# A graph-network kernel on one core: degree sums taken from the attention's tiles, twelve adjacency tiles kept, x loaded in pieces, key loads with other strides

## The chip, the cores and the metric

The kernel runs on one core of a Trainium2 chip. The time is the device time of one execution in microseconds, and what counts is the median of several runs.

## The reference, cut to what matters

Four layers work on 3327 nodes with 128 features and one adjacency matrix of zeros and ones. Each layer takes the layer norm of x, clips it at zero and adds its result to x.

- Layer 0: `x1 = swish((adj @ h) @ W + b)`, then the same once more with x1 in place of h. Two products with the whole adjacency.
- Layer 1: attention with 128 heads of 8 features: `softmax(q k^T * scale + adj + adj)`, times v, and an output projection. The adjacency is added twice, so the kernel adds its double.
- Layer 2: `adj @ states`, a message layer and a GRU cell.
- Layer 3: a normalised product with `d = 1 / sqrt(sum(A, axis=-1))`, distances between all nodes, the four nearest, and a second normalised product. Only here are the sums of the adjacency, the degrees, needed.

## The kernel before

Nodes stand in T = 26 slots of P = 128 partitions (`NP` = 3328, one more than N = 3327). The adjacency is read as its transpose `adjT`: tile t holds 128 source nodes (127 in the last tile) and a row of 3327 destination nodes, 1.7 MB in float32. A sum over a node's neighbours is therefore a sum over partitions and tiles.

The front of the program and the attention each stand in a manual schedule: every engine's instructions, and the DMA issues on SP's queue, keep the order in which the program writes them. PE is TensorE, DVE is VectorE, ACT is ScalarE, POOL is GpSimd, and SP issues DMAs.

**Layer 0.** `load_x` (L95) brings x in three DMAs by groups of partitions. Layer norm goes over three pieces of slots (`cuts`, L331) in stages `centre`, `spread`, `scaled`, and splits h into two float16 parts. The first product (L410 to L421) loads the 26 tiles through three buffers (`load_a`), multiplies both parts with the upper 16 bits of the tile (L373), and calls `look_at` (L401): DVE adds the tile to `colsum` (L405), and ACT sums the lower 16 bits of each number (L407). Ten tiles, `KEPT` (6, 8, ... 24), are also cast to bfloat16 by ACT (L419) and stay in SBUF. For half of them DVE collects all bits into `most` (`every_bit`).

The second product (L455 to L484) runs over `order`: the loaded tiles, with a kept tile after every two. Each loaded tile is read by PE, by DVE for its greatest value (`a_max`, L465), and by POOL, which writes its first 476 columns, doubled and in bfloat16, for the attention (`doubled`, L270 to L278). Between these stand seven products of ones with `colsum` (L477), copied by ACT into a row, which goes to DRAM and back as `deg` (one degree per partition and slot). In its midst SP loads x once more, with nodes in another order (`x_r`, L482 to L484). Four kept tiles, `TAIL`, are multiplied last, column chunk by column chunk.

**Projections.** `project_rows` (L616) runs over 26 blocks of rows and stores q, k and v in DRAM. From the fifth block on, a list `early` of steps is worked off beside it: raw loads of the keys of the first two head groups (`load_raw`, L688), one DMA for each head, whose rows are copied four times; queries and values; their parting into a rounded part and a rest (`split_rows`, whose sign and zero pattern comes from bits 8 and 16 of the partition number, L745); and the first tiles' exponentials.

**Attention.** Queries go in seven chunks of 476 columns (`q_chunks`, `QW`), heads in 32 groups of four, and keys in 26 tiles. The loop (L869 to L911) has one step per chunk c, group g and tile t; a tile pair shares one buffer `p8`. For an even tile PE makes four score products in the four `early` banks (L816), and DVE adds the doubled adjacency to them (L819). For an odd tile three products go to `late`, one of which PE also adds the adjacency to (L835), and the fourth to an `early` bank and DVE. ACT takes the exponential of the three (L837); POOL multiplies two of them by the exponential of the adjacency (L839); ACT takes the exponential of the other five (L840). `weigh` multiplies with the values six steps later (L847), and at a group's last tile DVE copies the result to `o4` (one buffer, L856), which four DMAs store. `key_pair` copies two tiles of keys (L603) on DVE at each odd tile but one.

The doubled tiles of chunk c + 1 are made while chunk c runs. At step t = 6 SP loads the next of the 26 tiles (`load_adj`), in at most one group a tile; at step t = 22 POOL doubles it (L908), after that step's scores in the program's order:

```python
if t == max(T - 4, 3) and c + 1 < len(q_chunks):
    for a, i, w in a_in:
        a_next.append(doubled(adj_pools[(c + 1) % 2], a[: rows_of(i), :w], i, w))
        to_store.append((c + 1, i, a_next[-1]))
```

`tail` (L984) holds layers 2 and 3 and the attention's output projection; `deg` is first used at L1030. A second, general path (L1289 on) runs only where the data do not fit the fast one; it does not run here.

## Time and profile before

| | |
|---|---|
| median of 3 runs | 10946.24 us (10944.75 to 10950.41) |
| profiled execution | 10958.07 us |
| its span, first to last instruction | 10956.4 us |
| busy PE / DVE / ACT / POOL | 97% / 95% / 93% / 66% |
| front: layer 0 and projections | 0 to 486 us |
| attention | 486 to about 10200 us |
| output projection, layers 2 and 3 | the rest |
| L819, adds of the adjacency on DVE | 14560 times, 646 ns each |
| L840, exponentials of five tiles on ACT | 2912 times, 2633 ns |
| L837, exponentials of three tiles on ACT | 2912 times, 1801 ns |
| L839, products on POOL | 2912 times, 2173 ns |
| L603, copies of keys on DVE | 2681 times, 552 ns |

A line of a timeline gives the start in us, the duration, the engine, the line of the kernel, the operation, what it writes and reads, and how often it is repeated; in brackets stands how long the engine was idle before it, and who ended that. Durations of instructions that follow each other on one engine overlap, so the distance between their starts is what each one costs. A line of windows gives start and end, the length, the busy time of PE, PE's weight loads, DVE, ACT and POOL with the number of instructions, the granted TensorE clock as a share of the full one, the DMA share and the GB/s.

### The profile page before, as it was taken

What the parts mean: (1) busy time and instruction counts of PE and PEld (TensorE: products, weight loads), DVE (VectorE), ACT (ScalarE), POOL (GpSimd) and SP (SyncE); (2) the same over time, 40 slices, a digit from 0 to 9 for tenths busy, and PEclk for the clock granted to TensorE, in tenths of its full rate; (3) what the DMA queues carried; (4) which work ended last, traced back from release to release, by engine and by line L of the source; (5) the groups of instructions that cost most, each with busy time, mean ns of one, the idle gap of its engine ahead of it and who ended that gap; (6) DMA issues with size and microseconds to landing.
All of it is one profiled execution on the core that took longest, in us unless ns stands there. A gap on an engine that the chain in (4) does not pass through costs nothing.

```text
span 10956.4 us, 201911 instructions
## 1 busy us (share of the span) xinstructions
PE 10591.0 (97%) x76701; PEld 3116.0 (28%) x76740; DVE 10354.7 (95%) x18137; ACT 10140.6 (93%) x6324; POOL 7260.8 (66%) x4298
## 2 busy tenths in 40 slices
PE   6899999999999999999999999999999999999897
PEld 2322222222222222222222222222222222222453
DVE  7699999999999999999999999999999999999665
ACT  4599999999999999999999999999999999999432
POOL 2278887777777777777777777777777766666203
PEclk8999999999999999999999999999999999999998
DMA  7655555433433433433343343343333333333422
GB/s 275 206 123 128 125 120 118 69 63 67 70 63 64 70 65 64 70 65 63 69 68 63 64 70 64 64 71 63 62 68 67 62 61 63 56 62 59 149 99 99
DMA packets 420289, 928.18 MB, mean 85 GB/s; under 512 B 67713, under 2 KB 349201, under 8 KB 385004
## 3 DMA queue, kind: packets, MB, share of 16 engines
q1 hardware_dynamic: 416058, 908.63, 40.7%
q8 instruction: 606, 9.93, 0.4%
q0 software_dynamic: 3248, 6.53, 0.2%
q14 instruction: 377, 3.09, 0.1%
HBM read 775.17 MB, written 139.72 MB: 84 GB/s over the span
## 4 chain that ended last, share of the span: by engine, by line
ACT 74%; issue 9%; PE 9%; DVE 3%; POOL 1%; DMA 1%; SPq 0%; DVEq 0%; ACTq 0%; POOLq 0%
ACT p L837 44%; ACT p L840 28%; PE acc L847 3%; DVE p L819 1%; PE agg_ps L228 1%; PE early L816 1%; ACT e L519 1%; PE late L816 1%; PE late L835 1%; PE yp L1026 0%; POOL rows L1242 0%; DVE idx L1218 0%; DVE top L1217 0%; SPq L593 0%; ACT oT L1023 0%
## 5 line engine op out<-in xcount | busy, mean ns | idle before, releaser
L819 DVE TENSOR_TENSOR p<-early,a 128x476 f32<-128x476 f32 (+1 forms) x14560 | 8414.3, 646 | 115.2 <-PE early L816 83.6
L839 POOL TENSOR_TENSOR p<-p,e 128x952 f32<-128x952 f32 (+2 forms) x2912 | 6326.6, 2173 | 2653.5 <-ACT p L837 2247.5
L840 ACT ACTIVATE p<-p 128x2380 f32<-128x2380 f32 (+1 forms) x2912 | 7667.2, 2633 | 0.0
L847 PE MATMUL acc<-p,v 128*9 128x476 f32 (+1 forms) x46592 | 5739.6, 564 | 22.4 <-DVE o L856 5.5
L837 ACT ACTIVATE p<-late 128x1428 f32<-128x1428 f32 (+1 forms) x2912 | 5243.6, 1801 | 20.7 <-PE late L835 19.0
L816 PE MATMUL early<-q,k 32*128 32x476 f32 (+1 forms) x14560 | 3714.1, 479 | 27.3 <-DVE p L819 8.2
L816 PEld LDWEIGHTS early<-q,k 32*128 32x128 f32 x14560 | 1579.4, 181 | 2752.6 <-DVE p L819 2690.1
L603 DVE CAST k<-k_in 128x256 fp32r<-128x256 f32 x2681 | 1479.3, 552 | 0.0
L816 PE MATMUL late<-q,k 32*128 32x476 f32 (+1 forms) x8736 | 1416.4, 479 | 52.0 <-ACT p L837 51.9
L816 PEld LDWEIGHTS late<-q,k 32*128 32x128 f32 x8736 | 547.5, 181 | 2378.2 <-ACT p L837 2265.5
L835 PE MATMUL late<-a,two_i 128*128 128x476 bf16 (+1 forms) x3072 | 1124.0, 374 | 0.0
L847 PEld LDWEIGHTS acc<-p,v 128*9 128x9 f32 x46592 | 692.6, 88 | 1347.5 <-issue 1257.5
L835 PEld LDWEIGHTS <-two_i 128*128 128x128 bf16 x3072 | 281.0, 96 | 665.1 <-issue 665.1
L228 PE MATMUL agg_ps<-a,part 128*128 128x512 bf16 (+1 forms) x1067 | 242.2, 379 | 49.4 <-issue 43.1
L373 PE MATMUL agg_ps<-a,part 128*128 128x512 bf16 (+2 forms) x714 | 175.6, 402 | 87.0 <-DMA a<-in_adjT_dram 63.0
L187 ACT COPY agg<-agg_ps 128x512 f32<-128x512 f32 x9 | 4.7, 594 | 255.8 <-PE agg_ps L228 255.8
L277 POOL TENSOR_SCALAR a<-a_in 128x476 bf16<-128x476 f32 (+2 forms) x156 | 240.0, 1539 | 0.5
L603 POOL CAST k<-k_in 128x256 fp32r<-128x256 f32 x231 | 203.1, 880 | 0.0
L1211 PE MATMUL sp<-yT,hT 128*128 128x512 f32 (+1 forms) x364 | 170.6, 610 | 12.4 <-ACT agg L1216 6.5
L228 PEld LDWEIGHTS <-part 128*128 128x128 f16 x1092 | 109.5, 101 | 177.1 <-issue 76.0
L1127 POOL TENSOR_TENSOR xs_late<-xs_late,b_s 128x3328 f32<-128x3328 f32 x1 | 7.3, 7252 | 227.4 <-DVE ln_xc L157 227.4
L856 DVE COPY o<-acc 105x476 f32<-105x476 f32 (+1 forms) x224 | 144.7, 646 | 6.6 <-PE acc L847 5.8
(284 smaller groups left out, 2615.8 us busy)
## 6 DMA issues: line engine op xcount, KB each, us to landing
k_in<-kt SPq DMA_DIRECT2D x1776, 207.9 KB
v<-vd SPq DMA_DIRECT2D x896, 117.0 KB
a<-in_adjT_dram SPq DMA_DIRECT2D x40, 1663.5 KB
a<-adj SPq DMA_DIRECT2D x78, 831.8 KB
q<-qt SPq DMA_DIRECT2D x1520, 29.8 KB
a_in<-in_adjT_dram SPq DMA_DIRECT2D x125, 238.0 KB
adj<-a SPq DMA_DIRECT2D x156, 119.0 KB
vd<-v_st SPq DMA_DIRECT2D x25, 576.0 KB
```

The lines of the kernel that those rows point to most:

```text
L228: nc.tensor.matmul(acc[c][:, :w], part[:, t, :], a[:, c0 : c0 + w], start=(t == 0 and i == 0), stop=(t == T - 1 and i == len(parts) - 1),)
L277: nc.gpsimd.tensor_scalar(a2[:kp, :w], a, 2.0, None, op0=ALU.mult)
L373: nc.tensor.matmul(acc[c][:, :w], part[:kp, t, :], a16[:kp, c0 : c0 + w], start=(n == 0 and i == 0), stop=(last and i == len(parts) - 1),)
L603: engine.tensor_copy(k, slots(k_in)[:, t : t + 2, :])
L816: nc.tensor.matmul(sp[:, :we], k[r, t % 2, :], q4[r, :we], start=True, stop=stop)
L819: nc.vector.tensor_tensor(p8[:, PLACES[t % 2][i], :we], sp[:, :we], a2[:, :we], op=ALU.add)
L835: nc.tensor.matmul(late[:, i, :we], two_i, a2[:, :we], start=False, stop=True)
L837: nc.scalar.activation(p8[:, 5:8, :we], late[:, :, :we], AF.Exp)
L839: nc.gpsimd.tensor_tensor(g8, g8, e_a[:, :we].unsqueeze(1).to_broadcast([P, n_g, we]), op=ALU.mult)
L840: nc.scalar.activation(p8[:, :5, :we], p8[:, :5, :we], AF.Exp)
L847: nc.tensor.matmul(acc[32 * i : 32 * i + EA, :w], v4[:kp, i, t, :], p8[:kp, PLACES[t % 2][i], :w], start=(t == 0), stop=(t == T - 1),)
L1211: nc.tensor.matmul(sp[:, c0 : c0 + w], slots(zT)[:, t, :], z2T[:, cols], start=True, stop=False)
```

## The change

- The degrees are no longer summed from the float32 tiles in layer 0. `add_to_sum` adds each doubled tile to `deg_half` [128 x 476]. For chunk 0 POOL does it, during the second product, right after each doubling. For chunks 1 to 6 DVE does it, right after the doubling in the attention's step t = 22 (the first tile of each chunk is copied by POOL instead). `store_sum` multiplies ones with `deg_half`, halves the row and writes it to DRAM: for chunk 0 in the second block of the projections, for chunk c at step t = 5 of its own first group, through an `early` bank and an `o4` buffer. `deg` is read back at the beginning of `tail` in the program; in SP's queue the load stands in the second group of the last chunk.
- `KEPT` has twelve tiles (2, 4, ... 24). `a_max` of the other fourteen and `every_bit` of all twelve are taken by DVE in the first product. In the second product DVE reads no tile. 14 tiles are loaded there instead of 16.
- The first three loads of the second product stand ahead of everything else, the loads of `x_r` follow them at once, and the fourth load comes after these.
- `load_x` goes by pieces of slots (0 to 2, 2 to 8, 8 to 26), which the first layer norm takes too.
- `load_raw` writes a head's eight rows with the four copies of each row next to each other, and a step of the list loads all four heads of a group; the sign pattern takes bits 1 and 2. The list has 16 steps instead of 22.

The general path keeps a sum of its own, which is left out below.

```diff
--- before.py
+++ after.py
@@ -92,10 +92,14 @@
     tiny_c = const.tile([P, 1], F32, name="tiny_c")
     nc.vector.memset(tiny_c, 1e-10)
 
+    X_CUTS = (0, 2, 8, T)
+
     def load_x(dst):
         nc.vector.memset(dst[96:P, T - 1, :], 0.0)
-        for p0, p1, n in ROW_PARTS:
-            nc.sync.dma_start(dst[p0:p1, :n], dram(x_in, p0 * T * D, [[T * D, p1 - p0], [D, n], [1, D]]))
+        for t0, t1 in zip(X_CUTS, X_CUTS[1:]):
+            for p0, p1, n in ROW_PARTS if t1 == T else ((0, P, t1),):
+                n = min(n, t1) - t0
+                nc.sync.dma_start(dst[p0:p1, t0 : t0 + n], dram(x_in, (p0 * T + t0) * D, [[T * D, p1 - p0], [D, n], [1, D]]))
 
     weights = const
 
@@ -277,6 +281,22 @@
         nc.gpsimd.tensor_scalar(a2[:kp, :w], a, 2.0, None, op0=ALU.mult)
         return a2
 
+    degd = dpool.tile([1, NP], F32, name="degd")
+    deg_half = const.tile([P, QW], F32, name="deg_half")
+
+    def add_to_sum(engine, a2, c, first=False):
+        w = q_chunks[c][1]
+        if first:
+            nc.gpsimd.tensor_copy(deg_half[:, :w], a2[:, :w])
+        else:
+            engine.tensor_tensor(deg_half[:, :w], deg_half[:, :w], a2[:, :w], op=ALU.add)
+
+    def store_sum(c, dp, row):
+        q0, w = q_chunks[c]
+        nc.tensor.matmul(dp[:1, :w], ones, deg_half[:, :w], start=True, stop=True)
+        nc.vector.tensor_scalar_mul(row[:1, :w], dp[:1, :w], 0.5)
+        nc.sync.dma_start(degd[:, q0 : q0 + w], row[:1, :w])
+
     def node_quad(agg, ps, y, t0, n, scale=1.0):
         mp = ps.tile([P, 4, D], F32, name="mp")
         for j in range(n):
@@ -294,7 +314,7 @@
 
     PART = 4096.0
     X_PART = 512.0
-    KEPT = list(range(6, T, 2))
+    KEPT = list(range(2, T, 2))
     TAIL = KEPT[:4]
     CS = chunks(N, 512)
 
@@ -328,7 +348,7 @@
         xc = ln.tile([P, T, D], F32, name="ln_xc")
         sq = ln.tile([P, T, D], F32, name="ln_sq")
         mean, var, rstd = (ln.tile([P, T], F32, name=f"ln_{name}") for name in ("mean", "var", "rstd"))
-        cuts = (0, 4, 12, T)
+        cuts = X_CUTS
 
         def centre(p, n):
             nc.vector.tensor_reduce(mean[:, p], xs[:, p], AX.X, ALU.add)
@@ -358,8 +378,6 @@
 
     right = ctx_st.enter_context(tc.tile_pool(name="l1_keep", bufs=1, side="right"))
     kept_pool = ctx_kept.enter_context(tc.tile_pool(name="l0_kept", bufs=len(KEPT)))
-    colsum = pool.tile([P, NP], F32, name="colsum")
-    nc.gpsimd.memset(colsum[:, N:NP], 0.0)
     most = pool.tile([P, NP // 2], I32, name="most")
     nc.gpsimd.memset(most, 0)
     junk = right.tile([P, T, D], F32, name="x_r").rearrange("p t d -> p (t d)").bitcast(BF16)
@@ -399,10 +417,6 @@
         nc.vector.tensor_scalar(dst, dst, 1000.0, 2.0, op0=ALU.mult, op1=ALU.add)
 
     def look_at(a, t, kp):
-        if t == 0:
-            nc.vector.tensor_copy(colsum[:, :N], a)
-        else:
-            nc.vector.tensor_add(colsum[:kp, :N], colsum[:kp, :N], a[:kp])
         low = a.bitcast(U16).rearrange("p (n two) -> p n two", two=2)[:kp, :, 0]
         nc.scalar.activation(junk[:kp, :N], low, AF.Copy, accum_out=low_bits[:kp, t : t + 1])
 
@@ -417,8 +431,9 @@
             kept[t] = kept_pool.tile([P, NP], BF16, name="a16")
             nc.gpsimd.memset(kept[t][:, N:], 0.0)
             nc.scalar.copy(kept[t][:kp, :N], a[:kp])
-            if len(kept) <= len(KEPT) // 2:
-                every_bit(kept[t])
+            every_bit(kept[t])
+        else:
+            nc.vector.tensor_reduce(a_max[:kp, t : t + 1], a[:kp], AX.X, ALU.max, apply_absolute_value=True)
 
     agg = new_agg(pool)
     for c in (6, 5, 4, 3, 2, 1, 0):
@@ -448,47 +463,36 @@
             between = between[1:]
     assert sorted(order + TAIL) == list(range(T))
     firsts = [None] * T
+    early_a = [load_a(t) for t in order[:3]]
+    nc.vector.memset(x_r[96:P, T - 1, :], 0.0)
+    nc.sync.dma_start(x_r[:, : T - 1], dram(x_in, 0, [[D, P], [P * D, T - 1], [1, D]]))
+    for p0, p1 in ((0, 112), (112, P - 1)):
+        nc.sync.dma_start(x_r[p0:p1, T - 1], dram(x_in, ((T - 1) * P + p0) * D, [[D, p1 - p0], [1, D]]))
     acc = new_acc()
-    deg_row = pool.tile([P, NP], F32, name="agg")
-    degd = dpool.tile([1, NP], F32, name="degd")
-    sums = chunks(NP, 512)
     for n, t in enumerate(order):
         kp = rows_of(t)
         if t in kept:
             part_products(acc, n, parts1, t, kept[t], range(len(CS)), False)
             src = kept[t][:kp, : q_chunks[0][1]]
-            if t in KEPT[len(KEPT) // 2 :]:
-                every_bit(kept[t])
         else:
-            a = load_a(t)
+            a = early_a.pop(0) if early_a else load_a(t)
             part_products(acc, n, parts1, t, words(a)[:, :, 1], range(len(CS)), False)
-            nc.vector.tensor_reduce(a_max[:kp, t : t + 1], a[:kp], AX.X, ALU.max, apply_absolute_value=True)
             src = a[:kp, : q_chunks[0][1]]
         firsts[t] = doubled(adj_pools[0], src, t, q_chunks[0][1])
+        add_to_sum(nc.gpsimd, firsts[t], 0, n == 0)
         if n == 0:
             nc.vector.tensor_reduce(x_max, x1.rearrange("p t d -> p (t d)"), AX.X, ALU.max, apply_absolute_value=True)
         if n == 1:
+            at_most(a_max[:, TAIL[0] : TAIL[0] + 1])
             nc.gpsimd.dma_start(vd[N * NH : N * NH + 1, :], zero[:1, :EA])
             for end in (qf, kf):
                 nc.gpsimd.dma_start(end[:E, N * NH :], zero[:E])
-        if 2 <= n < 2 + len(sums):
-            c0, w = sums[n - 2]
-            dp = ps0.tile([P, 512], F32, name="mp")
-            nc.tensor.matmul(dp[:1, :w], ones, colsum[:, c0 : c0 + w], start=True, stop=True)
-            nc.scalar.copy(deg_row[:1, c0 : c0 + w], dp[:1, :w])
-        if n == 2 + len(sums):
-            nc.gpsimd.dma_start(degd, deg_row[:1])
-        if n == 6:
-            nc.vector.memset(x_r[96:P, T - 1, :], 0.0)
-            nc.sync.dma_start(x_r[:, : T - 1], dram(x_in, 0, [[D, P], [P * D, T - 1], [1, D]]))
-            nc.sync.dma_start(x_r[: P - 1, T - 1], dram(x_in, (T - 1) * P * D, [[D, P - 1], [1, D]]))
-    at_most(a_max[:, TAIL[0] : TAIL[0] + 1])
     for t in TAIL:
         firsts[t] = doubled(adj_pools[0], kept[t][:, : q_chunks[0][1]], t, q_chunks[0][1])
-    nc.gpsimd.dma_start(deg, degd.rearrange("o (p t) -> (o p) t", t=T))
+        add_to_sum(nc.gpsimd, firsts[t], 0)
     a_first += firsts
     agg = new_agg(pool)
-    y = pool.tile([P, T, D], F32, name="colsum")
+    y = pool.tile([P, T, D], F32, name="h")
 
     def mp_rows(c, mp):
 
@@ -685,8 +689,9 @@
         nc.vector.tensor_copy(hi[:, :w], src[:, :w])
         nc.vector.scalar_tensor_tensor(dst[:, :w], hi[:, :w].bitcast(F32), low, src[:, :w], op0=ALU.mult, op1=ALU.add)
 
-    def load_raw(dst, src, g, i, w):
-        nc.sync.dma_start(dst[32 * i : 32 * i + 32, :w], dram(src, (4 * g + i) * N, [[0, 4], [GP, E], [1, w]]))
+    def load_raw(dst, src, g, w):
+        for i in range(4):
+            nc.sync.dma_start(dst[32 * i : 32 * i + 32, :w], dram(src, (4 * g + i) * N, [[GP, E], [0, 4], [1, w]]))
 
     assert 7 * N + NP <= 2 * P * NH
     early = []
@@ -694,17 +699,15 @@
     for g in range(2):
         raw = {}
 
-        def keys(i, g=g, raw=raw):
-            if i == 0:
-                raw["k"] = kq.tile([P, NP], F32, name="k_in")
-                nc.gpsimd.memset(raw["k"][:, N:], 0.0)
-            load_raw(raw["k"], kf, g, i, N)
+        def keys(g=g, raw=raw):
+            raw["k"] = kq.tile([P, NP], F32, name="k_in")
+            nc.gpsimd.memset(raw["k"][:, N:], 0.0)
+            load_raw(raw["k"], kf, g, N)
 
         def others(g=g, raw=raw):
             w = q_chunks[0][1]
             raw["q"] = side.tile([P, QW], F32, name="q_raw")
-            for i in range(4):
-                load_raw(raw["q"], qf, g, i, w)
+            load_raw(raw["q"], qf, g, w)
             raw["v"] = load_values(g)
 
         def parted(g=g, raw=raw):
@@ -714,7 +717,7 @@
             first.append((q4, raw["v"]))
             k_ins.append(raw["k"])
 
-        early += [lambda i=i, keys=keys: keys(i) for i in range(4)] + [others, parted]
+        early += [keys, others, parted]
     ahead_part = Parting(2)
     early.append(lambda: (ahead_part.load(0), ahead_part.load(1)))
     early += [lambda: (key_pair(nc.gpsimd, k_ins, pairs), key_pair(nc.gpsimd, k_ins, pairs))] * (KEYS_AHEAD // 2)
@@ -742,7 +745,7 @@
             low_rows = []
             row = side.tile([P, 1], I32, name="row")
             nc.gpsimd.iota(row, pattern=[[0, 1]], base=0, channel_multiplier=1)
-            for bit in (E, HL):
+            for bit in (1, 2):
                 odd = side.tile([P, 1], I32, name=f"odd{bit}")
                 nc.vector.tensor_scalar(odd, row, bit, None, op0=ALU.bitwise_and)
                 low = side.tile([P, 1], F32, name=f"low{bit}")
@@ -754,6 +757,9 @@
                 early.pop(0)()
         if r % 2 and r // 2 < len(CS):
             store_x(r // 2)
+        if r == 1:
+            store_sum(0, ps.tile([P, 512], F32, name="tp"), l1.tile([1, QW], F32, name="deg_row", bufs=1))
+            nc.sync.dma_start(degd[:, N:], ones[:1])
 
     mx = side.tile([P, 5], F32, name="mx")
     for i, m in enumerate((q_max, k_max, a_max, low_bits, x_max)):
@@ -776,7 +782,6 @@
         nc.vector.tensor_scalar(fits[:, i : i + 1], value, limit, None, op0=op)
     nc.vector.tensor_reduce(unsafe, fits, AX.X, ALU.min)
     nc.vector.tensor_scalar(unsafe, unsafe, -1.0, 1.0, op0=ALU.mult, op1=ALU.add)
-    nc.vector.tensor_add(deg[:, T - 1 : T], deg[:, T - 1 : T], last_row)
     ctx_st.close()
     ctx_order.close()
 
@@ -895,6 +900,8 @@
                             ahead_part.load(0)
                             ahead_part.load(1)
 
+                if t == 5 and g == 0 and c:
+                    store_sum(c, ps.tile([P, 512], F32, name="early", bufs=4), a_pool.tile([P, QW], F32, name="o4"))
                 if t % 2 and len(pairs) < len(steps) // 2:
                     key_pair(nc.gpsimd if t == ahead - 1 else nc.vector, k_ins, pairs)
                 if t == 14 and n + 1 < len(groups):
@@ -906,6 +913,7 @@
                 if t == max(T - 4, 3) and c + 1 < len(q_chunks):
                     for a, i, w in a_in:
                         a_next.append(doubled(adj_pools[(c + 1) % 2], a[: rows_of(i), :w], i, w))
+                        add_to_sum(nc.vector, a_next[-1], c + 1, i == 0)
                         to_store.append((c + 1, i, a_next[-1]))
                 if t % 2 and g == n_groups - 1 and c + 1 < len(q_chunks):
                     e_next.append(exp_of(a_next[t], c + 1))
@@ -1027,6 +1035,8 @@
                     nc.vector.tensor_add(xs[:kp, t, :], xs[:kp, t, :], yp[:kp])
                     done(t + 1)
 
+            if not general:
+                nc.sync.dma_start(deg, degd.rearrange("o (p t) -> (o p) t", t=T))
             d1 = inv_sqrt(pool, deg, "d1")
             d1_in, d1_out = d1, d1
             if not general:
...
```

More of the change, by code (lines that the diff above doesn't have):

```diff
@@ L1293, with add_rows @@
             done(T)
+            colsum = pool.tile([P, NP], F32, name="colsum")
+            nc.vector.memset(colsum, 0.0)
+            def add_rows(t, kp, a):
+                nc.vector.tensor_add(colsum[:kp, :N], colsum[:kp, :N], a[:kp])
             for src in (h, None):
                 agg = new_agg(pool)
-                adj_matmul(agg, src or y)
+                adj_matmul(agg, src or y, add_rows if src else None)
                 y = pool.tile([P, T, D], F32, name="y")
@@ L1302 @@
             nc.gpsimd.dma_start(x1d, xs)
+            with tc.tile_pool(name="g0_dps", bufs=1, space=PSUM) as ps:
+                dp = ps.tile([P, T], F32, name="dp")
+                for i in range(T):
+                    nc.tensor.matmul(dp[:, i : i + 1], slots(colsum)[:, i, :], ones, start=True, stop=True)
+                nc.vector.tensor_copy(deg, dp)
+            nc.vector.tensor_add(deg[:, T - 1 : T], deg[:, T - 1 : T], last_row)
         with tc.tile_pool(name="g1", bufs=1) as pool, tc.tile_pool(name="g1_st", bufs=2) as st, tc.tile_pool(
```

## The prediction

> **What bounds the kernel now.** I read the chain of waits first, then the busy time by stage, then the instructions in order of time around the places that the change touches. The chain, by engine and by line:
>
> ```profile
> ACT 74%; issue 9%; PE 9%; DVE 3%; POOL 1%; DMA 1%; SPq 0%; DVEq 0%; ACTq 0%; POOLq 0%
> ```
>
> The windows (us, then busy PE, PEld, DVE, ACT, POOL; clock; DMA share; GB/s) are one group of the attention, the second adjacency product, and the whole attention:
>
> ```profile
> 5000.00:5043.00 43.00, 42.83 (x329) 11.56 (x325) 42.22 (x79) 43.00 (x28) 31.49 (x16) 1.00 0.39 68
> 187.00:286.00 99.00, 80.64 (x352) 34.25 (x358) 78.76 (x35) 6.13 (x11) 41.79 (x30) 0.93 0.70 259
> 486.00:10200.00 9714.00, 9617.26 (x72758) 2594.03 (x72758) 9602.05 (x17434) 9696.79 (x5889) 7039.88 (x4083) 1.00 0.40 73
> ```
>
> 89% of the span is attention: 224 groups of 26 key tiles, about 43.3 us each. ACT has no idle time in it, and PE and DVE are each within a microsecond of full. A wait added there costs the whole time unless it fits into that microsecond, and it comes back at every place where it is put.
>
> The next lines, from the timelines of DVE, ACT, POOL and PE in one group of the second query chunk, show the place where the change puts its add:
>
> ```profile
> 3366.26 2.89 DVE L819 TENSOR_TENSOR p<-early,a 128x476 f32<-128x476 f32 x5
> 3369.07 0.62 DVE L603 CAST k<-k_in 128x256 fp32r<-128x256 f32 x1
> 3368.35 2.09 ACT L837 ACTIVATE p<-late 128x1428 f32<-128x1428 f32 x1
> 3369.59 2.92 ACT L840 ACTIVATE p<-p 128x2380 f32<-128x2380 f32 x1
> 3371.67 2.10 ACT L837 ACTIVATE p<-late 128x1428 f32<-128x1428 f32 x1
> 3367.19 2.23 POOL L839 TENSOR_TENSOR p<-p,e 128x952 f32<-128x952 f32 x1 [1.11 <-ACT p L837]
> 3369.39 1.56 POOL L277 TENSOR_SCALAR a<-a_in 128x476 bf16<-128x476 f32 x1
> 3370.93 2.22 POOL L839 TENSOR_TENSOR p<-p,e 128x952 f32<-128x952 f32 x1
> 3368.87 0.82 PE L816 MATMUL early<-q,k 32*128 32x476 f32 x4
> ```
>
> These are tiles 22 and 23. The five DVE adds start 0.56 us apart and last 0.65: the fourth ends at 3368.59, the fifth (tile 23) at 3369.15, and ACT's L840, which needs it, starts at 3369.59. The doubling L277, which the program issues at tile 22, stands on POOL behind a multiply and ends only at 3370.95. In time it is 2.35 us behind the DVE instruction that it precedes in the program. Nobody minds today: the tile is for the next chunk.
>
> **The adds in the attention.** For each doubled tile of the next chunk, 26 in each of six chunks, the change puts one DVE add (deg_half += a2) right behind the doubling. The first tile of a chunk is copied on POOL, so 150 adds are left, 125 of them while chunks 1 to 5 run and 25 during chunk 0. The instruction order of the changed kernel shows each add behind the four adds of tile 22 and ahead of the fifth (tile 23), waiting for POOL. Behind it on DVE queue the fifth add, for which L840 waits, and all that follows. As work it is 0.56 us, the spacing of L819, and DVE has about that (L840 starts 0.44 us after the fifth add here). As a wait it is not covered:
>
> - DVE is free at 3368.6 and stands until the doubling ends at 3370.95.
> - POOL's multiply L839 is ready by then and starts at 3370.93. The add has two SBUF operands, and such an add has been held by POOL before:
>
> ```profile
> 33.23 3.58 POOL L347 TENSOR_TENSOR part<-h,part 128x1792 f16<-128x1792 f32 x1 [3.68 <-ACT part L346]
> 33.27 14.34 DVE L405 TENSOR_TENSOR colsum<-colsum,a 128x3327 f32<-128x3327 f32 x3
> ```
>
> Three adds took 14.34 us where one alone takes 3.62 (48.16 on the same timeline): the first waited out POOL's operation. So I let the new add wait for L839's end, 3370.93 + 2.22 = 3373.15. A cast held in this way ends 0.27 us after POOL although it takes 0.40 alone, so an add of 0.65 ends about 0.5 after, at 3373.65, and the fifth add 0.56 later, at 3374.2, which is 5.1 us late. Less the 0.5 us of slack, ACT stands for 4.6 us.
>
> - PE stands too: its fourth product of the next pair uses the bank that the fifth add frees, so it idles for nearly 5 us after 3369.3. The trace has a small case of just this chain, in chunk 0: a DVE cast held by POOL for two multiplies.
>
> ```profile
> 643.07 3.02 DVE L603 CAST k<-k_in 128x256 fp32r<-128x256 f32 x1
> 641.44 4.38 POOL L839 TENSOR_TENSOR p<-p,e 128x952 f32<-128x952 f32 x2
> 646.70 0.47 PE L816 MATMUL early<-q,k 32*128 32x476 f32 x1 [1.69 <-DVE p L819]
> 647.60 1.36 ACT L837 ACTIVATE p<-late 128x1428 f32<-128x1428 f32 x1 [2.23 <-PE late L835]
> 652.74 1.36 ACT L837 ACTIVATE p<-late 128x1428 f32<-128x1428 f32 x1 [1.63 <-PE late L835]
> 657.04 1.36 ACT L837 ACTIVATE p<-late 128x1428 f32<-128x1428 f32 x1 [0.86 <-PE late L835]
> 648.68:655.51 6.83, 6.78 (x33) 1.35 (x34) 4.10 (x9) 5.20 (x4) 3.58 (x2) 0.50 1.09 178
> ```
>
> A cast 2.6 us late cost ACT 2.23 us at once, and another 1.63 + 0.86 = 2.5 us because PE, after 1.69 us of idling, ran 6.83 us at clock 0.50. PE needs 3.1 of the 3.3 us of a pair at full clock, so at half it bounds. After a longer gap a part of the slow stretch falls into the gap itself: I take 1.8 us, between 0 and 2.5.
>
> Per add 4.6 + 1.8 = 6.4 us: 125 x 6.4 = 800. In chunk 0 the doubling ends only 1.5 us after the fourth add (median of its groups), 0.85 less: 3.8 + 1.8 = 5.6, and 25 x 5.6 = 140.
>
> The Trainium skill ("TensorE: Matmul & The Clock Gate", on the thin-M case) asks for no PE gap above about 3.4 us. The row above lost the clock after 1.69 us. For gaps of 5 us both give the drop; should the port not hold the add, the gap would be about 3 us, and the rule would put no clock loss there, the row one of 1.8. A second page ("SBUF — State Buffer", on the two sides) speaks against the change outright: VectorE with two SBUF inputs and GpSimd exclude each other for a whole instruction, and who starts first wins. If the add won, its share would fall to that of the first rival below.
>
> **Six store_sums** (tile 5 of a chunk's first group): a product of ones with deg_half (L477 has 1.02 us for 512 columns), then a DVE row into o4, which has one buffer, just filled and being stored by four DMAs. Behind it wait the DVE adds of tile 6. No row shows that wait; between 1 us (the product alone) and 9 us I take 5, nearest to a short DMA: 6 x 5 = 30.
>
> **The front.** In the second product (187 to 286) two tiles are no longer reloaded, DVE no longer reads the loaded tiles (16 reductions of 3.6 us, L465, which held the three buffers), seven ones-products (1 us each) go, and x_r is loaded before the tiles and no longer blocks SP behind a DVE memset. PE idled 99 - 80.6 = 18.4 us here. POOL gets 26 adds: at L502's 1.26 us for 512 columns that is 1.2 each, with a doubling of 1.4 some 2.6 per tile, under PE's 3.0. x_r (1.7 MB at 390 GB/s, 4.4 us) now stands ahead of the fourth tile. Bounds 0 and -25; I take -12. First product: ACT, busy 106 of 124 us, gets two more casts of 2.95 and starts some 4 us earlier, since x comes in pieces; the column adds of 3.62 on DVE make room for reductions of 3.55: between -5 and +6, 0. Raw key loads: 8 x 426 KB are 13 us of DMA at the 258 GB/s of that stage; half as long or twice, -6 to +13; I take -3 for these, the fewer and earlier load steps included. deg is loaded during the last chunk: nothing. Sum -15.
>
> **Sum.** 800 + 140 + 30 - 15 = +955 us. The profiled execution took 10958.1 us (span 10956.4 and 1.7 around it), 11.8 above the median of the runs: 10958.1 + 955 - 11.8, about 11,900.
>
> **Rivals.**
> - DVE gets the port first. The add starts at about 3371.05, the fifth ends at 3372.26, 3.1 late; 2.6 + 1.8 = 4.4 per add, 3.6 in chunk 0: 550 + 90 + 15 = +655, 11,600. For it: semaphore and next POOL start are within 0.1 us. Against: POOL started 3370.93 without a gap, and the cast at 643 lost twice running. Chance 0.17.
> - POOL holds the port but PE keeps its clock: 4.6 x 125 + 3.8 x 25 + 15 = +685, 11,630. Against: the row of 648.68. Chance 0.10.
> - Neither: 2.6 x 125 + 1.85 x 25 + 15 = +386, 11,330. Chance 0.08.
> - The other side: the adds are free. If the doubling came out before DVE reaches the add, its 0.56 us would go into the 0.6 us of slack, and the front alone counts, at best 25 + 5 + 6 = 36 us: 10,910. It decides when POOL finishes the doubling 2.35 us earlier relative to DVE, which needs POOL not to have the multiply of tiles 20 and 21 before it; the order shows that it has. Chance 0.05, which I split between faster (0.03) and no change.
>
> Forecast 0.60. Its own bounds are no clock loss at some places and the full 2.5 at all: up to 125 x 7.1 + 25 x 6.3 + 80 = +1125, 12,070. The range from 11,480 to 12,080 takes in the first two rivals. About 0.2% (22 us) is what can be told from no change.
>
> **What would show it.** Right: new DVE adds whose releaser is POOL's doubling, 150 of them; L840 idle before, released by DVE, for over 4 us once per group; the granted clock of the attention below 1.00, and groups of 43.3 us grown to about 50. Wrong: groups of 43.3 to 44 us, or ACT still without idle time; or groups near 46 with the clock at 1.00 (the third rival). The second product should be some 12 us shorter.

## The result, and the profile after

The changed kernel takes 11868.64 us (median; 11865.93 to 11874.76) against 10946.25 us in the same comparison. The ratio is 1.0842, with a 95% interval from 1.0828 to 1.0856. The forecast was 11,900 us.

The groups of the profile's page that answer to the attention's lines (before, the two exponentials had no idle time ahead of them worth naming):

```profile
L845 ACT ACTIVATE p<-p 128x2380 f32<-128x2380 f32 (+1 forms) x2912 | 6718.7, 2307 | 544.7 <-DVE p L824 544.7
...
L842 ACT ACTIVATE p<-late 128x1428 f32<-128x1428 f32 (+1 forms) x2912 | 4309.4, 1480 | 355.5 <-PE late L840 342.6
L821 PE MATMUL early<-q,k 32*128 32x476 f32 (+1 forms) x14560 | 3758.1, 490 | 693.8 <-DVE p L824 665.6
...
L292 DVE TENSOR_TENSOR deg_half<-deg_half,a 128x476 f32<-128x476 f32 (+1 forms) x150 | 394.8, 2632 | 293.3 <-POOL a L281 293.3
```

The last column is the engine's idle time just before these instructions and who ended it. The 150 new adds wait for POOL's doubling, 293.3 / 150 = 1.96 us each, and then take 2.63 us where an add of 476 columns has 0.65. ACT, which hardly ever stood in the attention before, now stands 544.7 us ahead of the exponentials of five (L845, the old L840), released by DVE, and 355.5 us ahead of the exponentials of three (L842, the old L837), released by PE. These two together are 900 of the 922 us that the kernel lost. (L845's mean of 2307 ns against the old 2633 is no gain: the distance from its start to the next start is 2.08 us in undisturbed rows of both kernels: 3369.59 to 3371.67 before, 3685.94 to 3688.02 after.)

One such place on the timeline, tiles 22 and 23 of a group, from DVE, ACT, POOL and PE:

```profile
3685.61 2.33 DVE L824 TENSOR_TENSOR p<-early,a 128x476 f32<-128x476 f32 x4
3689.80 2.63 DVE L292 TENSOR_TENSOR deg_half<-deg_half,a 128x476 f32<-128x476 f32 x1 [1.86 <-POOL a L281]
3692.36 0.64 DVE L824 TENSOR_TENSOR p<-early,a 128x476 f32<-128x476 f32 x1
3688.02 1.40 ACT L842 ACTIVATE p<-late 128x1428 f32<-128x1428 f32 x1
3693.03 2.19 ACT L845 ACTIVATE p<-p 128x2380 f32<-128x2380 f32 x1 [3.61 <-DVE p L824]
3696.85 1.36 ACT L842 ACTIVATE p<-late 128x1428 f32<-128x1428 f32 x1 [1.63 <-PE late L840]
...
3701.14 1.36 ACT L842 ACTIVATE p<-late 128x1428 f32<-128x1428 f32 x1 [0.86 <-PE late L840]
3688.36 1.41 POOL L281 TENSOR_SCALAR a<-a_in 128x476 bf16<-128x476 f32 x1
3689.73 2.20 POOL L844 TENSOR_TENSOR p<-p,e 128x952 f32<-128x952 f32 x1
3693.05 0.76 PE L821 MATMUL early<-q,k 32*128 32x476 f32 x1 [4.26 <-DVE p L824]
```

DVE is done with the fourth add at 3687.94 and stands until the doubling ends at 3689.77. POOL's multiply starts at 3689.73, the add 0.07 us later, and the add ends only at 3692.43, 0.50 us after the multiply. The fifth add follows, and ACT and PE with it. PE had been idle for 4.26 us, and the clock falls:

```profile
3687.50:3690.00 2.50, 1.29 (x11) 0.19 (x4) 0.64 (x2) 1.93 (x2) 2.50 (x3) 1.00 0.00 0
...
3693.50:3697.00 3.50, 3.50 (x18) 0.65 (x21) 2.76 (x6) 1.87 (x2) 0.00 (x0) 0.50 0.00 0
...
456.00:11136.00 10680.00, 9934.95 (x72961) 2600.26 (x72965) 9880.23 (x17620) 9784.46 (x5902) 7009.67 (x4096) 0.95 0.37 66
```

(The seventh figure is the granted clock: 1.00, then 0.50 in the busy stretch after the gap; the third line is the whole attention, with 0.95 where 1.00 stood.) In the attention the clock was at one half for 997 us, in 156 stretches; before, for 13.7 us in two.

By stages, from the two traces: attention 10679.0 us against 9736.5 (+942.5), front 456.1 against 486.8 (-30.7), the rest 729.0 against 733.1 (-4): +908 in the span. Counted from its first DVE add to that of the next, a group with an add of the sums has 49.66 us (median of chunk 1), one without 42.59, the mean of chunks 1 to 5 is 48.4 where it was 43.4, and chunk 6, which has no adds, stays at 43.0.

### The profile page after: what moved, and what is told of

The parts are those of the page before. It is cut to its first block, busy times and chain, and to the rows that moved or that the text cites. A ratio compares the mean times of both kernels' runs of the same rounds, so it can differ in the third digit from the quotient of the medians.

```text
span 11864.1 us, 202078 instructions
## 1 busy us (share of the span) xinstructions
PE 10878.6 (92%) x76740; PEld 3113.4 (26%) x76740; DVE 10518.1 (89%) x18267; ACT 10209.0 (86%) x6321; POOL 7228.1 (61%) x4329
## 5 line engine op out<-in xcount | busy, mean ns | idle before, releaser
L845 ACT ACTIVATE p<-p 128x2380 f32<-128x2380 f32 (+1 forms) x2912 | 6718.7, 2307 | 544.7 <-DVE p L824 544.7
L852 PE MATMUL acc<-p,v 128*9 128x476 f32 (+1 forms) x46592 | 5972.1, 586 | 21.3 <-DVE o L861 2.1
L842 ACT ACTIVATE p<-late 128x1428 f32<-128x1428 f32 (+1 forms) x2912 | 4309.4, 1480 | 355.5 <-PE late L840 342.6
L821 PE MATMUL early<-q,k 32*128 32x476 f32 (+1 forms) x14560 | 3758.1, 490 | 693.8 <-DVE p L824 665.6
L821 PE MATMUL late<-q,k 32*128 32x476 f32 (+1 forms) x8736 | 1459.8, 494 | 35.8 <-ACT p L842 35.7
L607 DVE CAST k<-k_in 128x256 fp32r<-128x256 f32 x2681 | 1259.1, 470 | 0.0
L840 PE MATMUL late<-a,two_i 128*128 128x476 bf16 (+1 forms) x3072 | 1155.3, 385 | 0.0
L292 DVE TENSOR_TENSOR deg_half<-deg_half,a 128x476 f32<-128x476 f32 (+1 forms) x150 | 394.8, 2632 | 293.3 <-POOL a L281 293.3
L840 PEld LDWEIGHTS <-two_i 128*128 128x128 bf16 x3072 | 282.1, 96 | 692.1 <-issue 692.1
L607 POOL CAST k<-k_in 128x256 fp32r<-128x256 f32 x231 | 174.1, 755 | 0.0
```

The lines of the kernel that those rows point to most:

```text
L292: engine.tensor_tensor(deg_half[:, :w], deg_half[:, :w], a2[:, :w], op=ALU.add)
L607: engine.tensor_copy(k, slots(k_in)[:, t : t + 2, :])
L821: nc.tensor.matmul(sp[:, :we], k[r, t % 2, :], q4[r, :we], start=True, stop=stop)
L840: nc.tensor.matmul(late[:, i, :we], two_i, a2[:, :we], start=False, stop=True)
L842: nc.scalar.activation(p8[:, 5:8, :we], late[:, :, :we], AF.Exp)
L845: nc.scalar.activation(p8[:, :5, :we], p8[:, :5, :we], AF.Exp)
```

## The experiments

The theory: DVE waits for the doubling, is then held by POOL's multiply, and PE loses its clock in the gap. (The port is the prediction's word for what POOL's multiply holds while DVE's add stands.) The rivals: the add as work; the port alone; no part for the clock. Ratios are to the kernel before on the same chip.

**The adds left out** (`no_adds`).

```diff
-                        add_to_sum(nc.vector, a_next[-1], c + 1, i == 0)
+                        if i == 0:
+                            add_to_sum(nc.vector, a_next[-1], c + 1, True)
```

> Leaves out the 150 DVE adds of the attention (the sums of chunks 1 to 6 then hold their first tile alone, and each stored degree gets 16 added so that it stays positive). store_sum, the POOL copies and the whole front stay. Theory (the add waits for POOL's doubling and then for POOL's port, and PE loses its clock meanwhile; 6.3 us each): all of it goes, and what is left is the front, which starts the attention 31 us earlier than before, and six store_sums at 5 us: 10,940 to 10,960 us, no group of 49 us left, clock 1.00. Rival (the cost lies in the rest of the change): the time stays near 11,870.

Measured: 10941.83 us, ratio 1.0001 [0.9990, 1.0012]. So the 150 adds are the whole loss: 11868.6 - 10941.8 = 927 us, 6.18 us each (923 when each kernel is taken against the kernel before of its own comparison). What is left of the change, six stores of sums and a faster front, cancels out.

**The wait without the add** (`wait_only`).

```diff
-                        add_to_sum(nc.vector, a_next[-1], c + 1, i == 0)
+                        if i == 0:
+                            add_to_sum(nc.vector, a_next[-1], c + 1, True)
+                        else:
+                            nc.vector.tensor_copy(deg_half[:, :1], a_next[-1][:, :1])
```

> In place of each add DVE copies one column of the fresh doubled tile: it waits for the same doubling but has no second operand and almost no work (sums left out, 16 added as in the run without adds). Theory: the tile 23 add comes 2 us late instead of 4.5, ACT loses about 1.6 us and PE's gap is some 2.4 us, which costs the clock in some groups: 1.6 to 3.9 us each, 11,180 to 11,530 us. If even this copy has to have POOL's port, it waits out the multiply too: 11,750 to 11,850. Rival (the wait is nothing, the add's own 0.56 us is what DVE has no room for): as without adds, 10,940 to 10,960.

Measured: 11557.73 us, ratio 1.0564 [1.0533, 1.0595]; 616 us over the kernel without adds, 4.1 us for each copy. The rows of DVE, ACT, PE and POOL:

```profile
5095.41 0.15 DVE L919 CAST deg_half<-a 128x1 f32<-128x1 bf16 x1 [1.87 <-POOL a L281]
5095.48 0.64 DVE L824 TENSOR_TENSOR p<-early,a 128x476 f32<-128x476 f32 x1
5096.04 1.77 DVE L607 CAST k<-k_in 128x256 fp32r<-128x256 f32 x1
5096.16 2.19 ACT L845 ACTIVATE p<-p 128x2380 f32<-128x2380 f32 x1 [1.12 <-DVE p L824]
5099.82 1.36 ACT L842 ACTIVATE p<-late 128x1428 f32<-128x1428 f32 x1 [1.47 <-PE late L840]
5096.18 0.53 PE L821 MATMUL early<-q,k 32*128 32x476 f32 x1 [1.77 <-DVE p L824]
5095.35 2.20 POOL L844 TENSOR_TENSOR p<-p,e 128x952 f32<-128x952 f32 x1
```

The same wait of 1.87 us stands ahead of a copy of 0.15 us, which POOL's multiply did not hold; the key cast behind it was held instead (1.77 us, 0.40 where nothing is in its way). So the wait, with hardly any work behind it, is already two thirds of the loss: 172.5 / 150 = 1.15 us ahead of the exponentials of five (the page's idle time there), the rest behind them, where the late cast and the lost clock were not taken apart. PE gaps of 1.8 us (median of the 150; 1.77 in the row) were enough to lose the clock: 857 us at half, in 153 stretches. The upper end of what I had expected, 3.9 us, was 0.2 short.

**The port without the wait** (`port_only`): the add takes the tile of the running chunk, which has long been there.

```diff
-                        add_to_sum(nc.vector, a_next[-1], c + 1, i == 0)
+                        add_to_sum(nc.vector, a_next[-1] if i == 0 else a_t[t], c + 1, i == 0)
```

> The same adds at the same place, with the same two SBUF operands, but of the current chunk's tile 22, doubled a chunk ago: no wait for POOL's doubling (the sums are of the wrong tiles, 16 added). Theory: the add finds POOL's multiply of tiles 20 and 21 running until 0.8 us after the fourth add, ends 0.5 us after that, and makes the fifth 1.3 us late; less the slack of 0.5 that is 0.8 us each and no clock loss: 11,040 to 11,080 us. Rival (DVE's capacity): the add's 0.56 us alone, 10,940 to 10,970. Rival (the wait does not matter, the port is all): near 11,870.

Measured: 11009.98 us, ratio 1.0064 [1.0041, 1.0087], 0.45 us for each add, a little under what was expected.

```profile
5027.75 1.17 DVE L292 TENSOR_TENSOR deg_half<-deg_half,a 128x476 f32<-128x476 f32 x1
5026.18 2.23 POOL L844 TENSOR_TENSOR p<-p,e 128x952 f32<-128x952 f32 x1 [1.10 <-DVE p L824]
5028.38 1.86 POOL L281 TENSOR_SCALAR a<-a_in 128x476 bf16<-128x476 f32 x1
```

The multiply ends at 5028.41 and holds the add for 0.5 us. The add seems to hold POOL in turn: the doubling, queued behind the multiply, takes 1.86 us here (median of chunk 1) and 1.40 in the changed kernel. Without the semaphore the add meets only the end of the multiply ahead; with it, it is released just as the next one begins, and meets all of that one. Neither the port met in this way (0.45) nor the wait with a copy behind it (4.1, the held key cast in it) gives 6.18: the wait decides when the add meets POOL.

**PE kept busy in the gap** (`warm`, 11 repeats; `warm19`, the same with 19). Both keep the adds; PE repeats the three `early` products that are ready while the fourth waits for its bank.

```diff
+                for _ in range(again):
+                    for i in range(3):
+                        product(i, early[i])
                 for i in range(4):
                     product(i, early[i])
 ...
+                again = 11 if t == T - 2 and c + 1 < len(q_chunks) and any(i for _, i, _ in a_in) else 0
```

> The changed kernel whole, but in the step behind each add PE makes its first three score products eleven times more, into the same banks, about 4.5 us of work in the time in which it would stand. Theory: DVE's delay and ACT's stall of about 4.1 us stay, the clock stays at 1.00, and the 2.3 us that ACT lost to PE at half clock go: 150 x 2.3 = 345 us less, 11,500 to 11,560 us. Rival (the clock costs nothing, DVE alone sets the loss): 11,870 or a little more.

> Only change against the changed kernel: in the groups with an add, PE issues the first three score products of the pair after the add's tile 19 times more into the same banks (the same values again, 57 short row-group products, 0.24 us per trio, some 4.6 us), so that it has something to do while the fifth add is late; with 11 repeats (2.84 us) a gap of 1.95 us was left and the clock still fell in most groups. Theory (of the 6.2 us per add, 4.1 are the wait and some 2.3 come from the clock that PE loses in the gap): the clock stays at 1.00 in the attention and 150 x 2.0 to 2.3 us go: 11,520 to 11,570. Rival A (the 2.3 us after the first stall are not the clock but the queue on DVE and PE that has to be caught up): no change against 11 repeats, 11,770 or more. Rival B (the repeats themselves delay the fourth product): slower than 11,870.

Measured: 11 repeats 11773.85 us, ratio 1.0761 [1.0730, 1.0793]; 19 repeats 11546.96 us, 1.0552 [1.0533, 1.0571]. The first was too short, and told little: the repeats lasted 2.84 us and left a gap of 1.95 us (the row below; the median of the 150 is 1.94), and half clock remained for 625 us, in 136 stretches.

```profile
4229.23 2.84 PE L821 MATMUL early<-q,k 32*128 32x476 f32 x36
4234.02 0.48 PE L821 MATMUL early<-q,k 32*128 32x476 f32 x1 [1.95 <-DVE p L824]
```

The second nearly closed the gap (0.21 us in the row, 0.35 in the median of the 150):

```profile
5083.01 4.56 PE L821 MATMUL early<-q,k 32*128 32x476 f32 x60
5087.78 0.47 PE L821 MATMUL early<-q,k 32*128 32x476 f32 x1 [0.21 <-DVE p L824]
```

and on its page the two waits of ACT come apart (L848 and L845 are the L845 and L842 of the changed kernel):

```profile
L848 ACT ACTIVATE p<-p 128x2380 f32<-128x2380 f32 (+1 forms) x2912 | 6767.5, 2324 | 553.0 <-DVE p L824 553.0
...
L845 ACT ACTIVATE p<-late 128x1428 f32<-128x1428 f32 (+1 forms) x2912 | 4357.2, 1496 | 56.8 <-PE late L843 44.7
```

The first wait is as before the repeats, 553.0 against 544.7; the second goes from 355.5 to 56.8, and half clock from 997 us to 44. So the clock costs 11868.6 - 11547.0 = 322 us (316 with each taken against the kernel before of its own comparison), 2.1 us for each add, and the stall itself the other 4.0. Rival A, a queue that has to be caught up whatever the clock, falls.

**The adds on POOL** (`pool_adds`).

```diff
-                        add_to_sum(nc.vector, a_next[-1], c + 1, i == 0)
+                        add_to_sum(nc.gpsimd, a_next[-1], c + 1, i == 0)
```

> Only change against the changed kernel: the 150 adds of the attention are issued on POOL, right behind the doubling there, instead of DVE. Theory (the cost is the DVE queue's wait for POOL, and POOL has some 12 us per group without work): groups of 43.3 us again, DVE waits for nothing, the six stores of the sums (some 30 us) and the faster front (some -31) remain: 10,935 to 10,965, like the kernel with the adds left out (10,941.8). Rival (POOL's add of about 1.2 to 1.4 us holds the port or delays the next multiply, so that DVE's key casts or the weighing products come late): up to 1.4 us in each of 150 groups, 11,000 to 11,150.

Measured: 11030.65 us, ratio 1.0081 [1.0067, 1.0094]. The rival was right, at 0.6 us for each add:

```profile
3190.86 1.46 DVE L607 CAST k<-k_in 128x256 fp32r<-128x256 f32 x1
3188.77 1.10 POOL L292 TENSOR_TENSOR deg_half<-deg_half,a 128x476 f32<-128x476 f32 x1
3189.82 4.59 POOL L844 TENSOR_TENSOR p<-p,e 128x952 f32<-128x952 f32 x2
```

The add takes 1.10 us, and the multiply behind it stands 1.1 us later, just where DVE has its key cast, which took 1.46 us and not 0.40, as some 150 of these casts did (1.3 us or more). POOL's idle time was not free: where its work stands in time matters to DVE.

**The DVE add at another place** (`late_add`): behind the key cast of the group's last tile, three tiles later.

```diff
+                if t == T - 1 and c + 1 < len(q_chunks):
+                    for _, i, _ in a_in:
+                        add_to_sum(nc.vector, a_next[i], c + 1, i == 0)
 ...
-                        add_to_sum(nc.vector, a_next[-1], c + 1, i == 0)
```

> Only change against the changed kernel: the DVE add is issued at the group's last tile, behind that tile's key cast, instead of right behind the doubling at tile 22; the doubling is then long done, so DVE waits for no semaphore. Theory (place, not work, is what costs): the add is 0.56 us of DVE's work as in the kernel that added a tile long ready (0.45 us each there), sometimes held by a multiply of POOL: 10,960 to 11,050. Rival (any add with two SBUF operands is held by POOL's multiply of 2.2 us, wherever it stands, since POOL is busy three quarters of the time): 1.5 to 2.5 us each and the clock, 11,200 to 11,450.

Measured: 10955.49 us, ratio 1.0013 [1.0004, 1.0022], so 927 us shrink to some 14, under 0.1 us for each add, a little under the range that was expected.

```profile
5004.87 2.89 DVE L824 TENSOR_TENSOR p<-early,a 128x476 f32<-128x476 f32 x5
5007.99 0.64 DVE L292 TENSOR_TENSOR deg_half<-deg_half,a 128x476 f32<-128x476 f32 x1
5005.47 2.24 POOL L844 TENSOR_TENSOR p<-p,e 128x952 f32<-128x952 f32 x1
5008.56 2.23 POOL L844 TENSOR_TENSOR p<-p,e 128x952 f32<-128x952 f32 x1 [0.86 <-ACT p L842]
```

The tile has been there for 2.5 us, POOL's multiply is over at 5007.71, the next begins at 5008.56, and the add, 0.64 us, lies between them; all 150 took 0.63 to 0.67. The same instruction on the same engine costs 6.18 us or 0.1, by its place alone.

**The store of the sum later** (`best`, on the adds on POOL; `best2`, on the late adds).

```diff
-                if t == 5 and g == 0 and c:
+                if t == 12 and g == 0 and c:
```

> As the kernel with the adds on POOL, and the store of the sum (product of ones, DVE row, DMA) is issued at tile 12 of a chunk's first group instead of tile 5, when the four stores of the chunk's results out of the same buffer are long done. Theory (a store_sum cost 5 us because its row waits for these stores): five to six times 4 us less than with the adds on POOL alone, 10,910 to 10,935, faster than the kernel before by 0.1 to 0.3%. Rival (the cost is the product of ones on PE and the bank that it holds, wherever it stands): no difference, 10,935 to 10,965.

> The changed kernel with its DVE adds at the group's last tile and the store of the sum at tile 12 of a chunk's first group instead of tile 5. Theory (the two costs are separate and both go): 10,955 (late adds alone) less 30 (what the later store took from the kernel with the adds on POOL), 10,920 to 10,932, which is 0.1 to 0.2% under the kernel before. Rival (at tile 12 the DVE row falls on other work when the adds are on DVE): 10,945 or more.

At t = 5 of the changed kernel DVE's row waits for the stores out of `o4`, 2.7 us in the mean of the six:

```profile
2020.28 0.64 DVE L297 TENSOR_SCALAR o<-early 1x476 f32<-1x476 f32 x1 [2.64 <-DMA ot<-o]
```

Measured: 11000.22 us, 30.4 us less than with the adds on POOL alone, and 10925.99 us with the late adds, about 30 less than these alone. That is 5.1 us for each of six stores, all of which go: the first group of a chunk has 43.3 us in the last kernel, and in the changed one it had 48.8 to 49.2 (47.4 in chunk 6). (The absolute figure expected of `best` stood on 10,940 for the adds on POOL and was missed with that.) The last kernel is 0.14% faster than the kernel before, ratio 0.9986 [0.9977, 0.9995], which just leaves out 1, and some 940 us faster than the changed one; ACT no longer stands ahead of the exponentials of five (ahead of those of three 20.6 us, before 20.7), and PE keeps its clock:

```profile
L845 ACT ACTIVATE p<-p 128x2380 f32<-128x2380 f32 (+1 forms) x2912 | 6819.3, 2342 | 0.0
```

```profile
466.00:10209.00 9743.00, 9648.41 (x72953) 2606.69 (x72957) 9613.87 (x17620) 9726.98 (x5902) 7031.04 (x4096) 1.00 0.41 73
```

**Three parts of the front undone**, each on this last kernel.

```diff
# ten_kept
-    KEPT = list(range(2, T, 2))
+    KEPT = list(range(6, T, 2))
# x_whole: load_x by groups of partitions, as before, and
-        cuts = X_CUTS
+        cuts = (0, 4, 12, T)
# raw_outer
-            ... [[GP, E], [0, 4], [1, w]]
+            ... [[0, 4], [GP, E], [1, w]]
-            for bit in (1, 2):
+            for bit in (E, HL):
```

> As the kernel with late adds and the late store, with 10 tiles of adj kept in SBUF instead of 12 (two more are loaded again in the second product, two casts less on ACT in the first). Theory A (the second product's gain of 16.5 us comes mostly from the two tiles, as loads are what PE waits for there): second product 8 to 14 us longer, the time 6 to 14 us longer. Theory B (it comes from the readers that DVE lost and from the tiles of x moved ahead, and two more loads fit in): second product within 4 us, the first one a little shorter, the time within 4 us.

> As the kernel with late adds and the late store, with x loaded by rows in whole (all 26 slots at once) and the layer norm cut at 4 and 12 instead of 2 and 8, as before the change. Theory A (the pieces of x are what starts the first product 5 us earlier, and the whole front shifts): 4 to 9 us longer, first product starting near 20. Theory B (my prediction's: the first product is bound by ACT, so an earlier start is given back by its end): within 2 us.

> As the kernel with late adds and the late store, with the raw key and query loads in the old order (the copies outermost, and the two bits that go with it). Theory A (the prediction's: the order of the descriptors is worth about 3 us of the projections): 1 to 5 us longer. Theory B (copies innermost read the same 13 KB row four times running and help more): 6 to 13 us longer. Theory C: no difference within 1 us.

Measured: ten tiles 10927.17 us, x in whole 10927.01, against 10925.99: neither is told from nothing. With x in whole the first product starts at 20.0 us instead of 14.4 and ends at 154.9 instead of 155.4, so the early start is given back, as theory B had it (one profile each; ten profiles with this front end the first product between 149.7 and 158.3). With ten tiles the second product takes 94.1 us, with twelve 92.9 to 99.0 in ten profiles of kernels with this front; theory B again. The old order of the copies costs 15.4 us (10941.35 us, ratio to before 1.0002 [0.9993, 1.0011]), more than theories A and B gave. Ahead of the parting of the two groups' raw keys DVE stood 25.2 us for their loads with the old order and 11.6 with the new. In the projections of the last kernel, and then with the old order, PE stood:

```profile
L632 PE MATMUL pp<-w_st,hT 128*128 128x512 f32 (+1 forms) x104 | 56.9, 675 | 27.1 <-ACT qk_st L627 27.0
```

```profile
L632 PE MATMUL pp<-w_st,hT 128*128 128x512 f32 (+1 forms) x104 | 58.2, 689 | 38.2 <-ACT qk_st L627 38.0
```

that is 11 us of the 13.5 by which the projections grew (182.7 to 196.2 us). Undone is the order alone, not the new step that issues a group's four loads at once. The kernel before, with the old order and single steps, took 186.5, and DVE stood 0.2 us for these loads there. By subtraction the new step would cost some 10 us and the new order give 14; the step was not run by itself.

## Why the prediction was right

- **The 150 adds.** 800 + 140 = 940 us were forecast, 927 measured. The mechanism holds in each link: released by the doubling, held by the multiply, ended 0.5 us after it (predicted 0.5), the fifth add and ACT behind it, then the clock. Two sizes were off and partly made up for each other. The stall ahead of the exponentials of five is 544.7 / 150 = 3.6 us and not 4.6: the doubling ended 1.85 us after the fourth add (median of chunk 1) instead of 2.35, for it took 1.41 us instead of 1.56 and began 0.3 us earlier against that add, and what followed had 0.76 us of slack, not 0.5 (in the kernel with late adds the exponentials start 1.32 us after the fourth add, where the fifth ends at 0.56). The part behind it was larger than the 1.8 us I took out of 0 to 2.5: 355.5 / 150 = 2.4 us stand there; 38.3 of the 355.5 stand there without the adds too, which leaves 2.1, and the repeats took away 2.1. (3.6 + 2.1 are 5.7 of the 6.18; the other 0.4 was not traced.) In the row the trace gave me, 1.63 + 0.86 us stood after a gap of 1.69; I lowered it for longer gaps, and after 4.26 us the same 1.63 + 0.86 stand. In chunk 0 the doubling ended at 1.52 (predicted 1.5), the exponentials were 3.8 us late (predicted 3.8); but they were 3.8 us late in chunk 1 as well, the later doubling being made up for by the larger slack there, so that the predicted difference between chunk 0 and the others did not come.
- **The port.** The first rival, DVE first, is excluded by the rows: POOL starts 0.07 us ahead of the add, and 0.05 to 0.09 in all 150. That agrees with what the Trainium skill says of the port ("SBUF — State Buffer", on the two sides), that the first to start has it for the whole instruction. The rows of `wait_only` show that which DVE instruction is held is a matter of its form: the one-column copy (0.15 us) and the fifth add (0.64 us, one operand in PSUM) ran beside the multiply, the key cast did not.
- **The clock.** The second rival is excluded by the repeats (322 us). The skill's rule ("TensorE: Matmul & The Clock Gate", on oscillation), no gaps above some 3.4 us, is too lenient here: gaps of 1.8 us (median) lost the clock in 153 places, gaps of 0.35 us (median) did not. The window of 3413 ns that the same page states (on what is actually happening) agrees with the length of our slow stretches: of the 156 in the attention of the changed kernel 136 last 6.83 us and 20 last 3.41.
- **The stores of the sums.** 6 x 5 = 30 us forecast, from bounds of 1 and 9; 30.4 measured, and the reason (the stores out of `o4`) shows in the row and goes away with the place. That the 5 hit so closely is luck: no row gave it, only the bounds.
- **The front.** -15 us forecast, about -31 measured (without the adds the change came to -0.7 us in all, 30.4 of the stores among it). This term was off by as much as it is large. The first product ended 8.0 us earlier in the median of ten profiles with this front (149.7 to 158.3 us, against 160.9 in the one profile of before), where I had 0: ACT's two more casts did come (35.4 us of casts against 29.5), but its waits for loads fell from 14.9 to 7.5 us (6.2 to 11.8 in the ten), which I had not counted. With ten tiles kept they were 16.6 us, so that the two casts seem to fill time in which ACT would stand. What ends the first product earlier stays open, since with x in whole it ended no later. The second product took 95.1 us in the median of these, 14.7 less (I took 12): in the groups of PE, before and after,

```profile
L373 PE MATMUL agg_ps<-a,part 128*128 128x512 bf16 (+3 forms) x356 | 81.4, 385 | 20.3 <-DMA a<-in_adjT_dram 16.8 <-DVE h L434 3.0
L477 PE MATMUL mp<-colsum,ones 128*1 128x512 f32 (+1 forms) x14 | 6.7, 560 | 0.0
```

```profile
L391 PE MATMUL agg_ps<-a,part 128*128 128x512 bf16 (+3 forms) x364 | 81.0, 384 | 11.6 <-DMA a<-in_adjT_dram 9.5 <-DVE h L449 2.0
```

  the ones-products (6.7 us) are gone, and 7.3 us of waiting for loads (9.5 us are left in this profile, up to 12.9 in others with this front). Not for the reason I put first: two tiles less to load gave nothing that shows. That leaves the tiles' readers and `x_r` ahead of them, which I did not take apart. The projections took 182 us instead of 186.5, -4 where I had -3; if the subtraction above holds (-14 and +10), that is luck.

The sum of the misses, -13 for the adds and -16 for the front, is the 31 us between forecast and result, to within 2 us.

## What to carry to other kernels

An instruction put behind a producer on another engine costs the distance in time between the two engines at that place, and then whatever its release collides with; so look up in the timeline where both engines are when it is issued, not what it takes. Three tiles later the same add fell into a gap and cost nothing that mattered. And where PE is near full, a stall can cost half as much again in clock: here 4.0 us for the stall and 2.1 for the clock.

## What the runs showed that I had not expected

A wait for a busy engine's result aims the waiting instruction at that engine's next instruction: without the wait the add cost 0.45 us, and the wait with a trivial copy behind it 4.1, but together they took 6.18. A DVE copy of one column ran beside the POOL multiply that held a key cast (0.15 us against 1.77). And PE gaps of 1.8 us (median) lost the clock nearly as often as gaps of 4.3 (153 and 156 stretches), so halving the gap was no cure. It need not be closed wholly either: counted over nine traces of these kernels, a half-clock stretch began within 3.5 us of the end of 5 of 542 gaps of 0.75 to 1 us in the attention, of 10 of 35 of 1 to 1.5 us, and of 211 of 225 of 1.5 to 2 us.
